# State scan of a four-layer network: one scan instruction over a whole image instead of two over its halves

## The chip, the cores and the metric

The kernel runs on one core of a Trainium2 chip. The metric is the device time of one execution in microseconds (us). Three runs of the kernel before gave 5059.32, 5066.79 and 5072.86 us; the median is 5066.79. A separate, profiled execution gave the page and the trace from which all durations below are read.

Engine names as in the profile: PE is the matrix engine (PEld its weight loads), DVE the vector engine, ACT the scalar engine with the activation functions, POOL the general engine, SP the engine that here does nothing but issue DMA transfers. "SPq" is SP's queue of issues; ACT and POOL issue some transfers too. L863 is line 863 of the kernel.

## What is computed

The reference is a network of four layers on an input of 8 images, 384 channels, 32 x 32 pixels. The change touches layer 0, a bidirectional selective state scan, and the place where layer 1 of an image begins. Cut to that:

```python
u = silu(causal_conv4(u) + conv1d_b)                 # (B, L, C), L = 1024 pixels
delta = softplus(dt @ dt_proj_w.T + dt_proj_b)       # (B, L, C)
A = -exp(A_log)                                      # (C, 16)
deltaA = exp(delta[..., None] * A)                   # (B, L, C, 16)
deltaBu = (delta * u)[..., None] * Bm[:, :, None, :]
def step(h, inp):
    dA, dBu, c = inp
    h = dA * h + dBu
    return (h, einsum('bdn,bn->bd', h, c))
y = scan(step, 0, ...) + u * D_param
y = y * silu(z)
out = einsum('bld,od->blo', y, out_proj_w)
```

It is run once forward (`fwd`) and once on the flipped sequence (`bwd`); their sum, scaled, is added to x together with a gated 3 x 3 convolution. Layer 1 (a convolution block, linear attention and an MLP), layer 2 (seven depthwise convolutions) and layer 3 (a 13 x 13 depthwise convolution with a pointwise one) follow.

For each image and each direction there are 384 channels x 16 states x 1024 pixels of recurrence, `h = dA * h + dBu`.

## The kernel before

**Three stages.** The front of image 0 runs alone. Then comes the long stage, 4 ms of the 5: the scan of image b runs as a chain of rounds, and between the rounds the kernel puts pieces of other jobs, the front of image b+1 (`front`: norm, input projection, convolutions, delta) and layer 1 of image b-1 (`layer1`). Last come layer 1 of image 7 and the layers 2 and 3 for all images.

**The scan, `scan(b)`.** A tile has 128 partitions: 32 channels x 4 states. The unit of work is (d, h, c): direction d, half h of the pixels (512 of 1024), chunk c of 128 channels. There are 2 x 2 x 3 = 12 units an image, for d = 1 with the halves in the order 1, 0. A unit has four rounds r, one for every four of the 16 states, so an image has 48 rounds, and a round has two tiles i. A tile is 128 x 1024 and holds two groups of 32 channels side by side, 512 pixels each. For a tile:

- ACT makes `da = exp(dlt * neg_a)` (L846), once for each group, since the factor per partition differs: two instructions on 512 columns. `da` has N_DA = 4 buffers.
- DVE makes `du = vr * bct` (L851), one instruction on 1024 columns into PSUM; `bct` holds the rows B and C of four states for one half.
- DVE runs the recurrence with `tensor_tensor_scan` (L863), once for each group, from `da` and `du` into `hs` (N_HS = 8 buffers). In the first half it starts from 0; in the second it starts from a state kept in `carry`.
- in the first half, DVE copies the last state of both groups into `carry` (L868).
- POOL multiplies `hs` by the row C in place (L872).

**The sums, `sums`.** PE sums the four states of a channel with the matrix `selt`: four 32-column products a round, one for each group, into the PSUM bank `acc` (L552 for the first, L557 for the others). There is one such bank; ACT fills it with `y0` at the start of a unit (L803). In the profile each fp32 product is two records. The sums of round n are put into the program in round n+2, so two rounds wait in the list `late`; at the end of an image the list is emptied (`for un in late`). After round 3 of a unit ACT copies `acc` and stores it as `yf` (d = 0, L816, L817), or DVE multiplies it by `zr` (L819) and POOL issues the store to `g_d` (d = 1, L820). For d = 1, `y0` is what d = 0 stored.

**Loads of the scan.** All go through SP: for a unit `dlt` and `vr` in two tiles each, each tile in two transfers of 256 KB, one for a group (L792), with N_REP = 6 buffers of one tag; `y0` (L832), `zr` (L835), and `bct` (L778) whenever the half or the direction changes. A load waits in SP's queue until its buffer is free.

**Jobs between the rounds.** `jobs` holds for each job a cost and the rounds from which and to which it runs. After each round the kernel takes pieces (up to the next `yield`) of the job that is furthest behind, until none is. Layer 1 of image b may run from round `(b + 1) * rounds` to round `(b + 2) * rounds`; its first piece, which loads weights and inputs, is taken 8 rounds before the scan of image b ends. `layer1` begins with the out projection: for h = 1 and then h = 0 it loads `xx` and `g`, and multiplies (`op<-g,wo`). Each engine works through its instructions in the order that the scheduler of the kernel's language gives them; the program order is their priority.

Of the kernel before, what the change touches and what calls it, by code (L numbers as in the profile page):

```python
# [10 lines left out]
FP = mybir.dt.float32  # L11
# [30 lines left out]
N_REP, N_DA, N_HS = 6, 4, 8  # L42
# [365 lines left out]
def _layers01(tc, nc, B, xv, x2_d, dram, ident, mean_w, eps5, eps6, one, half, minus1, vec, bns, bnt,  # L408
# [12 lines left out]
    with ExitStack() as ctx:  # L421
# [76 lines left out]
        carry = wp.tile([P, NC * NR, 4], FP, tag="carry", name="carry")  # L498

# [257 lines left out]
        newest = []  # L757

        def scan(b):

            units = [
                (d, h, c)
                for d in range(2) for h in ((0, 1) if d == 0 else (1, 0)) for c in range(NC)
            ]
            late = []

            def pairs(t):
                return t.rearrange("p (j n) -> p j n", n=HALF)

            def load_bc(k, r):  # L770
                d, h, _ = units[k]
                t = scanp.tile([P, 2, HALF], FP, tag="bct", name=f"bct_{b}_{d}_{h}_{r}", bufs=4)
                for o in range(2):
                    src = bass.AP(
                        bc_d.tensor, bc_d[b, d, o * NST + 4 * r, h * HALF].offset,
                        [[0, 32], [L, 4], [1, HALF]],
                    )
                    nc.sync.dma_start(t[:, o, :], src)  # L778
                return t

            def load(k, i):

                d, h, c = units[k]
                ts = []
                for src_d, n in ((dl_d, "dlt"), (v_d, "vr")):
                    t = scanp.tile([P, 2 * HALF], FP, tag="rep", name=f"{n}_{b}_{d}_{h}_{c}_{i}", bufs=N_REP)
                    for j in range(2):
                        src = bass.AP(
                            src_d.tensor, src_d[b, d, P * c + 32 * (2 * i + j), h * HALF].offset,
                            [[L, 32], [0, 4], [1, HALF]],  # L790
                        )
                        nc.sync.dma_start(t[:, bass.ts(j, HALF)], src)  # L792
                    ts.append(t)
                return ts

            def sums(k, r, hs, made, acc, y0, zt):
                d, h, c = units[k]
                cols = bass.ts(h, HALF)
# [3 lines left out]
                elif r == 0:  # L802
# [4 lines left out]
                        hs[j // 2][:, bass.ts(j % 2, HALF)],  # L807
# [6 lines left out]
                if d == 0:  # L814
                    yt = s2(f"yt_{b}_{h}_{c}")
                    nc.scalar.copy(yt, acc)  # L816
                    nc.scalar.dma_start(yfv[b][:, c, cols], yt)  # L817
                else:
                    nc.vector.tensor_mul(zt, acc, zt)  # L819
                    nc.gpsimd.dma_start(gv[b][:, c, cols], zt)  # L820

            bct = [load_bc(0, r) for r in range(NR)]
            now = [load(0, i) for i in range(2)]
            acc = y0 = zt = nxt = None
            for k, (d, h, c) in enumerate(units):
                cols = bass.ts(h, HALF)
                second = k % (2 * NC) >= NC
                for r in range(NR):
                    if r == 0:
                        acc = accp.tile([P, HALF], FP, tag="acc", name=f"acc_{b}_{d}_{h}_{c}")  # L830
                        y0 = s2(f"y0_{b}_{d}_{h}_{c}")
                        nc.sync.dma_start(y0, (udv if d == 0 else yfv)[b][:, c, cols])  # L832
                    if r == 1 and d == 1:
                        zt = s2(f"zr_{b}_{h}_{c}")
                        nc.sync.dma_start(zt, zv[b][:, c, cols])  # L835
                    if r == 1 and k + 1 < len(units):
                        nxt = [load(k + 1, 0)]
                    hs, made = [], []
                    way = slice(None) if d == 0 else slice(None, None, -1)
                    end = HALF - 1 if d == 0 else 0  # L840
                    for i in range(2):
                        dlt, vt = now[i]
# [476 lines left out]
```

## Time and profile before

The profiled execution has a span of 5036.6 us between its first and its last instruction, 30.2 us less than the median of the runs.

| Stage (us from the span's start) | length | PE busy | DVE busy | ACT busy | POOL busy | granted PE clock |
|---|---|---|---|---|---|---|
| scan of image 1 (667 to 1154) | 487 | 428.8 | 425.1 | 315.7 | 333.1 | 0.92 |
| scan of image 2 (1154 to 1655) | 501 | 444.1 | 424.5 | 322.6 | 332.3 | 0.94 |
| scan of image 4 (2158 to 2660) | 502 | 442.9 | 423.2 | 323.1 | 332.4 | 0.94 |
| scan of image 5 (2660 to 3159) | 499 | 442.8 | 422.9 | 323.1 | 332.5 | 0.94 |
| scan of image 6 (3159 to 3644) | 485 | 435.5 | 419.1 | 311.9 | 332.0 | 0.94 |
| after the scans (4080 to 5037) | 957 | 803.0 | 378.5 | 165.2 | 329.9 | 0.93 |

The windows go from the first `du` multiply of an image to that of the next; images 0, 3 and 7 stand with the prediction. Busy time is the union of an engine's instructions. Matmuls overlap and their ends are modelled, so PE's busy time is somewhat more than what it needs. A group line of the page gives line, engine, operation, out<-in with shapes, count, then busy us and mean ns of one instruction, then the idle time of the engine just before such instructions and what ended most of it. A wait line gives who waited for whom: us in total, how many times, longest.

Of the transfers, by issue: `dlt<-dl_d` and `vr<-v_d` x384 each, 256 KB, landing 4.6 and 5.0 us (median) after issue; `bct<-bc_d` x256, 256 KB, 3.9 us; `g_d<-zr` on POOL's queue x48, 256 KB, 5.3 us; `g<-g_d` x16, 768 KB, 7.8 us. The 16 DMA engines are busy 68% of the time in the middle of the run.

### The profile page before, as it was taken

Reading aid. Unit: us, or ns where it says so; the run is one execution under the profiler, and the core shown is the slowest. Engines: PE = TensorE matmul, PEld = TensorE weight load, DVE = VectorE, ACT = ScalarE, POOL = GpSimd, SP = SyncE. Lnnn points to the kernel's source line nnn. Section 1 sums busy time; section 2 is a strip of 40 time slices with the busy share of each in tenths; the row PEclk is TensorE's granted clock in tenths of the full one; section 3 lists DMA queues with packets and bytes.
Section 4 is the critical chain, followed back from the end, with each engine's and each line's share of the span. In section 5 each row is a group of like instructions: output and inputs, shape, how many; then the busy total and the mean of one; then the engine's idle time right before and its main releaser. Section 6 shows DMA issues by size and latency. Waiting matters only on the chain. (4 is left out here: it accounts for less than half of the span.)

```text
span 5036.6 us, 58480 instructions
## 1 busy us (share of the span) xinstructions
PE 4203.6 (83%) x20128; PEld 1781.9 (35%) x20128; DVE 3791.7 (75%) x3861; ACT 2637.3 (52%) x3738; POOL 2997.3 (60%) x1546
## 2 busy tenths in 40 slices
PE   6466588888888888889888989889888879978988
PEld 2121223333333233323332333333333324457457
DVE  1599999878987898789978997889898830157256
ACT  2456555774577457745774577567645622200212
POOL 1477577666766676667666666766776760033058
PEclk9676799899989998999899989998988989999999
DMA  7976557577657765776577657765763672389798
GB/s 205 278 226 221 182 190 214 179 216 195 214 175 214 196 213 174 213 195 214 177 214 191 216 179 212 210 214 180 176 192 127 160 156 78 68 162 251 210 207 172
DMA packets 543120, 965.28 MB, mean 192 GB/s; under 512 B 56568, under 2 KB 220904, under 8 KB 542824
## 3 DMA queue, kind: packets, MB, share of 16 engines
q1 hardware_dynamic: 401648, 663.89, 45.1%
q0 software_dynamic: 58048, 205.76, 15.8%
q10 hardware_dynamic: 83128, 91.90, 6.7%
q8 instruction: 159, 2.61, 0.2%
q14 instruction: 137, 1.12, 0.1%
HBM read 726.36 MB, written 234.98 MB: 191 GB/s over the span
## 5 line engine op out<-in xcount | busy, mean ns | idle before, releaser
L872 POOL TENSOR_TENSOR hs<-hs,bct 128x1024 f32<-128x1024 f32 x768 | 2414.6, 3145 | 945.5 <-DVE carry L868 438.6
L846 ACT ACTIVATE da<-dlt,neg_a 128x512 f32<-128x512 f32 x1536 | 1035.8, 715 | 1041.4 <-DVE hs L863 970.7
L863 DVE TENSOR_TENSOR_SCAN hs<-da,carry,du 128x512 f32<-128x512 f32 x768 | 942.4, 1266 | 191.8 <-PE acc L557 139.1
L851 DVE TENSOR_TENSOR du<-vr,bct 128x1024 f32<-128x1024 f32 x768 | 1033.0, 1345 | 31.4 <-DMA vr<-v_d 19.6
L863 DVE TENSOR_TENSOR_SCAN hs<-da,du 128x512 f32<-128x512 f32 x768 | 900.9, 1208 | 129.3 <-PE acc L557 54.4
L557 PE MATMUL acc<-hs,selt 128*32 128x512 f32 x2304 | 541.5, 660 | 134.8 <-POOL hs L872 134.7
L539 PE MATMUL mf<-ln,w 128*128 128x512 f32 x1152 | 549.2, 623 | 27.6 <-DMA w<-w_d 17.0
L1172 PE MATMUL mo<-hm,w 128*128 128x512 f32 x1152 | 532.7, 600 | 15.0 <-DVE xx L1139 15.0
L552 PE MATMUL acc<-hs,selt 128*32 128x512 f32 x768 | 420.9, 643 | 58.6 <-POOL hs L872 50.3
L539 PE MATMUL in<-xn,win 128*128 128x512 f32 x576 | 292.4, 646 | 64.6 <-DMA win<-in_inproj_t 29.0
L539 PEld LDWEIGHTS mf<-ln,w 128*128 128x128 f32 x1152 | 222.8, 200 | 339.4 <-issue 271.9
L1172 PEld LDWEIGHTS mo<-hm,w 128*128 128x128 f32 x1152 | 214.5, 190 | 309.1 <-issue 281.3
L846 ACT ACT_TABLE_LOAD x235 | 301.5, 1283 | 7.1 <-DMA dw_i<-h_d 2.4
L330 PE MATMUL cv_a<-xt_a,tp_a 128*32 128x256 f32 x3072 | 183.8, 387 | 55.1 <-issue 26.6
L1142 POOL DMA_DIRECT2D x_d<-xx x48 | 56.5, 1179 | 282.1 <-DVE xx L1139 274.9
L539 PE MATMUL op<-g,wo 128*128 128x512 f32 x288 | 158.3, 701 | 73.8 <-DMA g<-g_d 73.8
L557 PE MATMUL dw<-dw_i,t3b 96*32 96x512 f32 x1056 | 203.9, 637 | 16.5 <-DMA dw_i<-h_d 16.1
L330 PE MATMUL cv_b<-xt_b,tp_b 128*32 128x256 f32 x3072 | 184.5, 393 | 38.3 <-DVE xt_b L306 25.7
L306 DVE COPY xt_b<-xt_b 32x2496 f32<-32x2496 f32 x96 | 149.2, 1554 | 68.0 <-DMA xt_b<-xp_d 63.4
L539 PEld LDWEIGHTS in<-xn,win 128*128 128x128 f32 x576 | 111.6, 204 | 237.1 <-issue 165.0
L330 PEld LDWEIGHTS cv_a<-xt_a,tp_a 128*32 128x32 f32 x3072 | 159.6, 138 | 79.6 <-issue 34.7
L330 PEld LDWEIGHTS cv_b<-xt_b,tp_b 128*32 128x32 f32 x3072 | 155.7, 139 | 67.4 <-issue 41.1
(196 smaller groups left out, 5758.8 us busy)
## 6 DMA issues: line engine op xcount, KB each, us to landing
dlt<-dl_d SPq DMA_DIRECT2D x384, 256.0 KB, 4.6
vr<-v_d SPq DMA_DIRECT2D x384, 256.0 KB, 5.0
bct<-bc_d SPq DMA_DIRECT2D x256, 256.0 KB, 3.9
ut<-u_d SPq DMA_DIRECT2D x192, 257.5 KB, 5.7
lc_i<-xn_d SPq DMA_DIRECT2D x192, 228.8 KB, 5.4
dw_i<-h_d SPq DMA_DIRECT2D x192, 228.8 KB, 5.4
w<-w_d SPq DMA_DIRECT2D x64, 576.0 KB, 6.1
w<-in_w SPq DMA_DIRECT2D x64, 576.0 KB, 5.7
```

The costliest lines, as they stand in the source:

```text
L306: nc.vector.tensor_copy(xt[at[e] : at[e] + e * H, :, 0 : RL - e - (e - 1)], xt[at[0] : at[0] + e * H, :, e : RL - (e - 1)],)
L330: nc.tensor.matmul(ps[H * e : H * (e + 1), 0:BW], tp[:, c, :].rearrange("p (j t) -> p j t", t=KT)[:, :, t], rhs, start=(t == 0), stop=(t = ...
L539: product = nc.tensor.matmul(ps, w[:, k, m * P : (m + 1) * P], rhs[k] if isinstance(rhs, list) else rhs[:, k, :], start=(k == 0), stop=(k ...
L552: first = product()
L557: tc.keep_in_program_order(product())
L846: nc.scalar.activation(da[:, bass.ts(j, HALF)], dlt[:, bass.ts(j, HALF)], AF.Exp, scale=neg_a[:, g, r : r + 1],)
L851: nc.vector.tensor_mul(pairs(du), pairs(vt), bct[r][:, 0:1, :].to_broadcast([P, 2, HALF]),)
L863: nc.vector.tensor_tensor_scan(t[:, s][:, way], da[:, s][:, way], du[:, s][:, way], k_c if second else 0.0, ALU.mult, ALU.add,)
L872: made.append(nc.gpsimd.tensor_mul(pairs(t), pairs(t), bct[r][:, 1:2, :].to_broadcast([P, 2, HALF])))
L1142: nc.gpsimd.dma_start(x2v[m, :, h * (H // 2) : (h + 1) * (H // 2), PADW + b * (W + PADW) : PADW + b * (W + PADW) + W,], rows(o),)
L1172: nc.tensor.matmul(acc[m], wb[:, f, m * P : (m + 1) * P], hm, start=(i == 0 and f == 0), stop=(i == FF // C - 1 and f == NC - 1),)
```

## The change

- A unit is now (d, c, q): direction, chunk c of 128 channels, and q, which half of that chunk's channels (64). It covers all 1024 pixels. There are again 12 units of four rounds with two tiles.
- A tile holds one group of 32 channels x 4 states over the whole image. One exp of 1024 columns and one scan of 1024 columns, always started from 0, replace two of 512; `carry` and its copies go.
- The exp writes into the `hs` tile, and the scan and POOL's multiply work on it in place; `da` goes. N_HS is 9 instead of 8, N_REP 5 instead of 6. `bct` tiles are twice as long.
- Loads: `dlt` and `vr` come as one transfer of 512 KB a tile. The four of the next unit are requested one in round 1 and the others in round 3, between the instructions that free their buffers. `bct` is loaded once a direction.
- The bank `acc` has the 64 channels' first half of the pixels in partitions 0 to 63 and their second half in 64 to 127, so `y0`, `zr`, `yf` and `g` move in two transfers of 64 partitions each (`fetch`, `keep`).
- The list of sums that wait, now `late_sums`, lives on from image to image and is emptied after the last image only.
- Layer 1 of an image may start 3 rounds later. It loads both halves of `xx` in its first piece, then `g` of the first two chunks, then `g` of the last chunk, and then multiplies for h = 1 and h = 0. In the last image the second piece is taken 3 rounds before the end.

```diff
-N_REP, N_DA, N_HS = 6, 4, 8
+N_REP, N_HS = 5, 9
...
-        newest = []
+        newest, late_sums = [], []
...
+            units = [(d, c, q) for d in range(2) for c in range(NC) for q in range(2)]
+            def halves(t_d, k):
+                _, c, q = units[k]
+                lo = P * c + 64 * q
+                return [t_d[b][lo : lo + 64, bass.ts(h, HALF)] for h in range(2)]
+            def fetch(t, t_d, k):
+                for h, src in enumerate(halves(t_d, k)):
+                    nc.sync.dma_start(t[64 * h : 64 * h + 64, :], src)
+            def keep(t_d, k, t, queue):
+                for h, dst in enumerate(halves(t_d, k)):
+                    queue.dma_start(dst, t[64 * h : 64 * h + 64, :])
...
+            def load(k, n):
+                d, c, q = units[k]
+                i, o = divmod(n, 2)
+                t = scanp.tile([P, L], FP, tag="rep", name=f"{('dlt', 'vr')[o]}_{b}_{d}_{c}_{q}_{i}", bufs=N_REP)
+                src_d = (dl_d, v_d)[o]
+                src = bass.AP(
+                    src_d.tensor, src_d[b, d, P * c + 64 * q + 32 * i, 0].offset, [[L, 32], [0, 4], [1, L]],
+                )
+                nc.sync.dma_start(t, src)
+                return t
...
-                        hs[j // 2][:, bass.ts(j % 2, HALF)],
+                        hs[j % 2][:, bass.ts(j // 2, HALF)],
...
                     for i in range(2):
+                        dlt, vt = now[2 * i : 2 * i + 2]
+                        t = scanp.tile([P, L], FP, tag="hs", name=f"hs_{b}_{k}_{r}_{i}", bufs=N_HS)
+                        nc.scalar.activation(t, dlt, AF.Exp, scale=neg_a[:, 4 * c + 2 * q + i, r : r + 1])
+                        if r == NR - 1 and more:
+                            nxt.append(load(k + 1, 2 * i + 1))
+                        du = accp.tile([P, L], FP, tag="du", name=f"du_{b}_{k}_{r}_{i}")
+                        nc.vector.tensor_mul(du, vt, bct[r][:, 0, :])
+                        if i == 0 and r == NR - 1 and more:
+                            nxt.append(load(k + 1, 2))
+                        if i == 0 and len(late_sums) > 1:
+                            late_sums.pop(0)()
+                        if i == 0 and k == per and r == 0:
+                            bct[NR - 1] = load_bc(1, NR - 1)
+                        nc.vector.tensor_tensor_scan(
+                            t[:, way], t[:, way], du[:, way], 0.0, ALU.mult, ALU.add,
                         )
+                        made.append(nc.gpsimd.tensor_mul(t, t, bct[r][:, 1, :]))
...
+                    late_sums.append(partial(sums, k, r, hs, made, acc, y0, zt))
...
-            for un in late:
-                sums(*un)
+            if b == B - 1:
+                while late_sums:
+                    late_sums.pop(0)()
...
             for h in (1, 0):
-                xh, gh = a6(f"xx_{b}_{h}"), a6(f"g_{b}_{h}")
-                nc.sync.dma_start(xh, x1v[b][:, :, bass.ts(h, HALF)])
-                nc.sync.dma_start(gh, gv[b][:, :, bass.ts(h, HALF)])
-                xx[h] = xh
-                yield 0
+                xx[h] = a6(f"xx_{b}_{h}")
+                nc.sync.dma_start(xx[h], x1v[b][:, :, bass.ts(h, HALF)])
+            yield 0
+            gh = {}
+            for h in (1, 0):
+                gh[h] = a6(f"g_{b}_{h}")
+                nc.sync.dma_start(gh[h][:, 0 : NC - 1, :], gv[b][:, 0 : NC - 1, bass.ts(h, HALF)])
+            yield 0
+            for h in (1, 0):
+                nc.sync.dma_start(gh[h][:, NC - 1, :], gv[b][:, NC - 1, bass.ts(h, HALF)])
+            yield 0
+            for h in (1, 0):
                 for m in range(NC):
...
-            jobs.append([seconds[b], 310, (b + 1) * rounds + 0, (b + 2) * rounds + 0, 0])
+            jobs.append([seconds[b], 310, (b + 1) * rounds + 3, min((b + 2) * rounds + 3, B * rounds), 0])
...
-                if i == rounds - 8:
+                if i == rounds - 8 or (b == B - 1 and i == rounds - 3):
                     next(seconds[b])
```

## The prediction

> **What bounds the kernel now.** I read the page's totals first, then a table of windows cut at the images (from the first du multiply of an image to that of the next), then the groups, then who waited for whom, and last the timelines at one change of image.
>
> ```profile
> span 5036.6 us, 58480 instructions
> ...
> PE 4203.6 (83%) x20128; PEld 1781.9 (35%) x20128; DVE 3791.7 (75%) x3861; ACT 2637.3 (52%) x3738; POOL 2997.3 (60%) x1546
> ```
>
> ```profile
> 146.00:667.00 521.00, 300.44 (x1079) 96.29 (x1078) 470.30 (x491) 275.06 (x381) 330.80 (x171) 0.72 0.69 216
> 1655.00:2158.00 503.00, 444.10 (x1696) 168.33 (x1696) 425.22 (x423) 323.04 (x447) 333.49 (x149) 0.94 0.68 199
> 3644.00:4080.00 436.00, 365.24 (x1263) 145.56 (x1260) 379.46 (x384) 233.10 (x341) 313.87 (x112) 0.90 0.53 150
> ```
>
> The columns are the window, its length, then busy time of PE, PEld, DVE, ACT and POOL, the granted clock, the DMA share and GB/s. The three rows are images 0, 3 and 7. Image 0 is DVE's (470 of 521 us, PE 300). In image 3, as in 1 to 6, PE (444) and DVE (425) are nearly level and both stand idle some 60 to 80 us. So the middle of the run is bound by two engines that take turns, and I ask at each saving who holds the path.
>
> ```profile
> L872 POOL TENSOR_TENSOR hs<-hs,bct 128x1024 f32<-128x1024 f32 x768 | 2414.6, 3145 | 945.5 <-DVE carry L868 438.6
> L846 ACT ACTIVATE da<-dlt,neg_a 128x512 f32<-128x512 f32 x1536 | 1035.8, 715 | 1041.4 <-DVE hs L863 970.7
> L863 DVE TENSOR_TENSOR_SCAN hs<-da,carry,du 128x512 f32<-128x512 f32 x768 | 942.4, 1266 | 191.8 <-PE acc L557 139.1
> L851 DVE TENSOR_TENSOR du<-vr,bct 128x1024 f32<-128x1024 f32 x768 | 1033.0, 1345 | 31.4 <-DMA vr<-v_d 19.6
> L863 DVE TENSOR_TENSOR_SCAN hs<-da,du 128x512 f32<-128x512 f32 x768 | 900.9, 1208 | 129.3 <-PE acc L557 54.4
> ```
>
> Of the waits in images 1 to 6 (667 to 3644 us), three decide:
>
> ```profile
> DVE hs L863 <- PE acc L557: 169.5, 54, 12.2
> ```
>
> ```profile
> PE op L539 <- DMA g<-g_d: 43.0, 5, 10.9
> PE acc L557 <- POOL hs L872: 40.7, 18, 2.8
> ```
>
> The scans wait 28 us an image for an hs buffer that PE's sums have not released. PE waits for the states only 7 us an image (the row above), but at each change of image it waits for g. The timeline of PE there:
>
> ```profile
> 1658.97 1.92 PE L557 MATMUL acc<-hs,selt 128*32 128x512 f32 x4 [2.79 <-POOL hs L872]
> ...
> 1667.84 5.31 PE L539 MATMUL op<-g,wo 128*128 128x512 f32 x12
> 1680.77 7.43 PE L539 MATMUL op<-g,wo 128*128 128x512 f32 x12 [7.62 <-DMA g<-g_d]
> ```
>
> The last sums of image 2 are emptied at its end, their g is written out (the issue on POOL is at 1662.01, SP's g load goes out at 1674.5), and PE stands behind that load.
>
> **Scans and carries (DVE).** Removed: 1536 scans of 512 and 384 carry copies (184 ns each); added: 768 scans of 1024. No row shows a scan of 1024. It can't cost more than two of 512 without carry, 2416 ns, and not less than that minus one whole smallest instruction, 2416 - 184 = 2232. DVE's instructions on 128x1 take 143 to 153 ns, which is nearly all fixed cost, so I take 2416 - 150 = 2266. Now a tile's two scans occupy
>
> ```profile
> 1653.01 2.45 DVE L863 TENSOR_TENSOR_SCAN hs<-da,carry,du 128x512 f32<-128x512 f32 x2
> 1655.50 1.23 DVE L851 TENSOR_TENSOR du<-vr,bct 128x1024 f32<-128x1024 f32 x1
> 1656.86 2.33 DVE L863 TENSOR_TENSOR_SCAN hs<-da,du 128x512 f32<-128x512 f32 x2
> ```
>
> 2.45 or 2.33 us, mean 2.39; less 2.27 is 0.12 us. A copy moves the next start by 0.08 us on half of the tiles, 0.04 more: 0.16 us a tile, 123 us over 768 tiles, 15.4 an image. What of it is on the path? I followed the chain of waits back from the last scan of each image, by the rule of the page's part 4: scans hold 150 us of the chain in image 0, 59 to 86 (mean 74) in images 1 to 6, 115 in image 7, of 237 us of scans each: 63%, 31% and 49%. So 15.4 x 0.63 + 6 x 15.4 x 0.31 + 15.4 x 0.49 = 9.7 + 28.6 + 7.5 = **46 us**. Bounds: 17 (images 0 and 7 alone) and 123 (all of it). The du multiply and POOL's multiply keep size and count.
>
> What speaks against it: POOL's multiply was released by the carry copy on half of the tiles (438.6 us of its waits) and is now released by the scan, just as the next du starts. Second-half tiles have no copy today, and there du takes 1.23 us (the fence above) while POOL's multiply stretches from 2.36 to 3.2 or 3.3: du goes first. I take nothing, and no loss as the bound.
> The Trainium skill ("SBUF — State Buffer", section "SBUF: two separate sides") says that a DVE instruction with two SBUF inputs and a GpSimd instruction exclude each other for their whole length, whoever starts first. By that rule alone a du that now came second would lose up to a whole POOL multiply, 384 x 2.36 = 906 us; the rows of the second halves show the other order, and the sum goes by them.
>
> **Exps (ACT).** 1536 of 512 become 768 of 1024. The Gelu rows, 475 ns at 256 and 687 at 512, give 0.83 ns a column, so 715 + 512 x 0.83 = 1139 instead of 1430: 0.29 us a tile, 223 us of ACT. On the same chains exps hold 22, 84 (six images together) and 25 us; 131 x 0.2 = 27 us. But they now write into hs, not into da, so exp n waits until PE's sums have freed tile n-9. In the trace a scan starts 13.3 us (median) after those sums, 4.7 at the tenth percentile, 3.2 at least, and the exp needs 1.2 of it. The 13.8 us by which exps lead today shrink. I take half, **13 us**; bounds 0 and 27.
>
> **Late sums and the shifted start.** The sums of an image's last two rounds no longer drain at its end, and the out projection starts 3 rounds later (some 31 us at 502/48 us a round), with g loaded in two parts ahead. PE's waits for g are 73.8 us in 8 places; the tail's one is 15.5, which leaves 58.3 for seven changes of image, 8.3 each. The chain runs on into DVE, whose L958 waits there 38.5 us in six images. I take all **58 us**. Bounds: 0 (another wait takes its place) and 58 plus the 3.6 us that PE waits for POOL's last tiles at this change (0.79 + 2.79), times 7: 83.
>
> **Tail.** In the last image the out projection of half 1 (18 records, 0.43 us apart in the timeline, 7.7 us) ran between the last sums, while half 0 waited for g. Now both wait for the last channel group: +7.7, less about 2 for a smaller last load (g 768 KB lands in 7.8 us, y 256 KB in 3.3 to 6.0): **+6 us**, bounds 0 and 8. Squeezing image 6's second layer into 45 rounds instead of 48 costs nothing while PE idles 70 of 436 us in image 7; 3/48 of its load (310 units, 3 for six records of 0.43 us: 17 us) would show if that idle time went.
>
> **Moves of data.** Per image SP issues 146 loads now and 100 then, the same bytes: dlt and vr in one piece of 512 KB, y and z in two pieces. Stores of yf and g are two pieces each: 48 more issues on POOL at 583 ns, 28 us, hidden in POOL's 170 idle us per image, and 48 on ACT's queue. With five rep buffers, dlt of a unit's second tile waits for the du of the last round's first tile, as vr of the second tile does today; that one landed a median of 10.7 us before its use and 3.6 at the tenth percentile, and dlt is wanted some 2.5 us sooner. So next to nothing, and behind it on SP stand the next vr and g. Buffers of N_HS and N_DA cost no time by themselves.
>
> **The sum.** -46 - 13 - 58 + 6 = -111 us, on a span of 5036.6: 4926. The median of the runs, 5066.8, lies 30.2 above that span, and that stays: **4956 us**. By the bounds: -123 - 27 - 83 + 0 = -233 and -17 + 8 = -9.
>
> **Rivals.** *All of it lands* (13%): PE's lag in images 1 to 6 comes from late DVE and ACT steps, so a lighter DVE frees PE too: 5066.8 - 233 = 4834. For it: DVE is 85% busy. Against: scans wait for PE, not PE for scans. *PE keeps the pace* (15%): images 1 to 6 stay as they are, the g wait is followed by a wait for an a6 buffer that the layer before still holds: 5066.8 - 17 - 4 + 6 = 5052. For it: POOL waits there 7.94 us for such a buffer. *Exps tied to the sums* (12%), the slower side: an exp that queues behind ACT's table load, Gelu and load back (1.28 + 0.69 + 1.28, some 3.3 us, and 1.2 of its own) comes too late where its slack is under 4.7 us, a tenth of the tiles. If a fifth of the tiles come 1.5 us late, 154 x 1.5 = 230, less 111: 5186. It decides from 74 tiles on, where 74 x 1.5 = 111. Against: the slack after n-9 today. That the long scan saves nothing is the lower bound of the first term.
>
> **How the numbers follow.** My forecast has 60%, with a range of its own of 4900 to 5010. About 0.3% (15 us, 5052 to 5082) is what a measurement can tell from no change. Faster: 60 + 13 and a third of PE's case, 78%; within 0.3%: 8%, most of PE's case; slower: 14%. The range leaves out half of the fastest case and most of the slow one: 4870 to 5080.
>
> **What would show it.** A scan row of 128x1024 near 2.27 us x768 and an exp row near 1.14; no carry row; DVE near 3600 us busy and ACT near 2410; the g wait of PE gone but for the tail, about 20 us there; image 0 near 511 and images 1 to 6 near 485 us. Wrong would be: long waits "DVE hs <- ACT" or "ACT <- PE acc", du far above 1.35 us, or g waits that reappear under another name.

## The result and the profile after

The changed kernel takes 5292.8 us (median of 4 runs, 5287.9 to 5294.0), the kernel before on the same chip 5069.8 (4 runs, 5059.3 to 5076.3). The ratio is 1.0439, 95% interval 1.0424 to 1.0454: **slower by 223 us**, where 111 us less were forecast.

The totals of the changed kernel's page:

```profile
span 5292.1 us, 55997 instructions
...
PE 4259.5 (80%) x20128; PEld 1782.4 (34%) x20128; DVE 3804.7 (72%) x2709; ACT 2439.9 (46%) x2936; POOL 3003.9 (57%) x1594
```

DVE runs 1152 instructions fewer and is busy for 3805 us, 13 more than before. ACT lost 197 us of work, of the 223 forecast. The groups say why DVE lost nothing (busy time and mean ns of one, then the idle time before them by cause):

```profile
L856 POOL TENSOR_TENSOR hs<-hs,bct 128x1024 f32<-128x1024 f32 x768 | 2400.5, 3126 | 1166.2 <-DVE hs L853 1048.3 <-issue 47.0 <-PE pj L537 10.6
L853 DVE TENSOR_TENSOR_SCAN hs<-hs,du 128x1024 f32<-128x1024 f32 x768 | 1754.6, 2285 | 392.4 <-ACT hs L842 334.8 <-PE dw L555 2.7 <-DVE du L846 1.4
L846 DVE TENSOR_TENSOR du<-vr,bct 128x1024 f32<-128x1024 f32 x768 | 1186.9, 1545 | 142.1 <-DMA vr<-v_d 122.2
L842 ACT ACTIVATE hs<-dlt,neg_a 128x1024 f32<-128x1024 f32 x768 | 851.8, 1142 | 421.1 <-DMA dlt<-dl_d 208.0 <-PE acc L555 194.3 <-issue 10.6
...
L537 PE MATMUL op<-g,wo 128*128 128x512 f32 x288 | 147.3, 653 | 124.7 <-DMA g<-g_d 124.7
```

The scan takes 2285 ns and the exp 1142 ns, close to the 2266 and 1139 that were worked out. But the du multiply, whose size did not change, went from 1345 to 1545 ns: 768 x 0.2 = 154 us. The scans and carries fell from 942.4 + 900.9 + 70.7 = 1914 us to 1754.6, which is 159 us. The one ate the other. And PE's wait for g rose from 73.8 to 124.7 us, where 58 of the 73.8 were to go.

The windows of images 0, 3 and 7 (length; busy time of PE, PEld, DVE, ACT, POOL; granted clock; DMA share; GB/s), cut at the first du multiply of each image as in the prediction:

```profile
173.00:668.00 495.00, 283.69 (x1005) 91.27 (x1006) 429.86 (x333) 220.37 (x249) 331.38 (x163) 0.68 0.68 214
1728.00:2271.00 543.00, 453.57 (x1698) 169.79 (x1697) 429.96 (x279) 303.22 (x351) 334.07 (x154) 0.90 0.63 184
3876.00:4323.00 447.00, 378.68 (x1300) 150.39 (x1299) 383.71 (x242) 212.86 (x249) 317.50 (x118) 0.91 0.52 147
```

Cut in this way, the whole difference of the two spans, 255.5 us, can be placed: the first du multiply starts 28 us later (173.7 against 145.8), image 0 is 27 us shorter, images 1 to 6 are 231 us longer together, image 7 is 11 and the rest 13 us longer. (The profiled execution of before was some 30 us under its median; hence 255 and not 223.) The shorter image 0 is no gain of the shorter scans: a unit now covers the whole image, so the first one needs both halves of the first front, and work of that front which ran between the rounds before now runs ahead of them. Image 1 begins at 668.0 us, before at 667.2. What the change cost, it cost where the layers run beside the scan: in image 3, 40 us, with PE busy 9 and DVE 5 us more. So most of it is waiting. The waits of images 1 to 6 (us in total, times, longest):

```profile
DVE hs L853 <- ACT hs L842: 295.8, 79, 21.7
ACT L842 <- PE acc L555: 167.1, 69, 7.2
...
ACT sq L641 <- DMA xi<-in_x: 123.5, 5, 26.8
...
PE ms_s L611 <- ACT sq L641: 107.7, 5, 22.3
DVE du L846 <- DMA vr<-v_d: 103.5, 15, 15.1
...
PE op L537 <- DMA g<-g_d: 96.3, 5, 21.4
```

Three things stand there that were not there before. Scans wait 296 us for their exps; exps wait for PE's sums; and five times, once an image, PE and ACT stand some 20 us behind `xi`, the input of the next front. In images 1 to 6 of the kernel before, these waits were:

```profile
DVE hs L863 <- ACT da L846: 12.6, 12, 1.5
...
PE ms_s L613 <- ACT sq L643: 10.6, 5, 3.2
...
ACT sq L643 <- DMA xi<-in_x: 9.4, 3, 4.0
```

The timeline of image 3 shows what a wait for `xi` drags along (start, length, and in brackets the idle time before it):

```profile
2191.39 2.37 POOL L1130 DMA_DIRECT2D x_d<-xx  x2
...
2194.55 1.16 POOL L1130 DMA_DIRECT2D x_d<-xx  x1 [0.80 <-issue]
...
2214.04 0.37 SPq L637 DMA_DIRECT2D xi<-in_x  x1
...
2219.45 1.67 ACT L641 ACTIVATE sq<-xi 128x512 f32<-128x512 f32 x3 [23.90 <-DMA xi<-in_x]
...
2220.13 1.17 PE L611 MATMUL ms_s<-sq,mean_w 128*32 128x128 f32 x16 [21.30 <-ACT sq L641]
...
2223.61 2.29 DVE L853 TENSOR_TENSOR_SCAN hs<-hs,du 128x1024 f32<-128x1024 f32 x1 [20.71 <-ACT hs L842]
```

The second layer (`layer1`), three rounds later now, stores its last result (`x_d<-xx`, three transfers) from an a6 buffer that the next front's `xi` is to take; a6 is the tag of the seven large tiles that the fronts and the layer share. The last of the three stores lands at 2213.89, 19 us after its issue. SP stands at the load of `xi` until then, 119.6 us in five times (20.1 in the kernel before), and vr and dlt of the next unit go out behind it (2214.5 to 2215.8). ACT stands at the squares of `xi`, with the exps of the scan queued behind them; PE stands at the mean, with the sums behind it; and so DVE and POOL stop too. One buffer that comes free too late stops all engines for 20 us.

### The profile page after: what moved, and what is told of

Its sections match the earlier page's. It is cut to its first block, busy times and chain, and to the rows that moved or that the text cites. A ratio compares the mean times of both kernels' runs of the same rounds, so it can differ in the third digit from the quotient of the medians.

```text
span 5292.1 us, 55997 instructions
## 1 busy us (share of the span) xinstructions
PE 4259.5 (80%) x20128; PEld 1782.4 (34%) x20128; DVE 3804.7 (72%) x2709; ACT 2439.9 (46%) x2936; POOL 3003.9 (57%) x1594
## 5 line engine op out<-in xcount | busy, mean ns | idle before, releaser
L853 DVE TENSOR_TENSOR_SCAN hs<-hs,du 128x1024 f32<-128x1024 f32 x768 | 1754.6, 2285 | 392.4 <-ACT hs L842 334.8
L846 DVE TENSOR_TENSOR du<-vr,bct 128x1024 f32<-128x1024 f32 x768 | 1186.9, 1545 | 142.1 <-DMA vr<-v_d 122.2
L842 ACT ACTIVATE hs<-dlt,neg_a 128x1024 f32<-128x1024 f32 x768 | 851.8, 1142 | 421.1 <-DMA dlt<-dl_d 208.0
L555 PE MATMUL acc<-hs,selt 128*32 128x512 f32 x2304 | 468.5, 679 | 118.9 <-POOL hs L856 118.9
L550 PE MATMUL acc<-hs,selt 128*32 128x512 f32 x768 | 435.0, 658 | 109.1 <-POOL hs L856 74.2
L537 PE MATMUL op<-g,wo 128*128 128x512 f32 x288 | 147.3, 653 | 124.7 <-DMA g<-g_d 124.7
L550 PEld LDWEIGHTS acc<-hs,selt 128*32 128x32 f32 x768 | 61.6, 114 | 371.2 <-issue 235.7
```

The costliest lines, as they stand in the source:

```text
L537: product = nc.tensor.matmul(ps, w[:, k, m * P : (m + 1) * P], rhs[k] if isinstance(rhs, list) else rhs[:, k, :], start=(k == 0), stop=(k ...
L550: first = product()
L555: tc.keep_in_program_order(product())
L842: nc.scalar.activation(t, dlt, AF.Exp, scale=neg_a[:, 4 * c + 2 * q + i, r : r + 1])
L846: nc.vector.tensor_mul(du, vt, bct[r][:, 0, :])
L853: nc.vector.tensor_tensor_scan(t[:, way], t[:, way], du[:, way], 0.0, ALU.mult, ALU.add,)
```

## The experiments

Each kernel starts from before or from after with the edit shown. "Before" ran on the same chip in each set; its median lay between 5066.7 and 5076.4.

### The shifted start

First the shift alone, in the kernel before:

```diff
-jobs.append([seconds[b], 310, (b + 1) * rounds + 0, (b + 2) * rounds + 0, 0])
+jobs.append([seconds[b], 310, (b + 1) * rounds + 3, min((b + 2) * rounds + 3, B * rounds), 0])
```

> The kernel before with one part of the change alone: layer 1 of an image may start, and must end, 3 rounds later. Theory S (the shift: the next front still begins 8 rounds before the scan's end and now finds its a6 buffers held by layer 1 of the image before, some 20 us an image in the trace of after): 5150 to 5220 us against 5070, with a wait of ACT sq for xi near 20 us an image. Theory E (exps tied to the hs buffers) or theory R (five rep buffers) as the main cause: within 0.5% of before, 5045 to 5095.

5290.6 us, ratio 1.0433 (1.0408 to 1.0459): by itself the shift costs as much as the whole change, 224 us, and more than was expected. In images 1 to 6 the wait for `xi` has come up:

```profile
PE ms_s L613 <- ACT sq L643: 108.7, 6, 21.9
```

Then the same with an eighth a6 buffer, for which room was made with fewer t2 and im buffers (smaller tiles of the fronts and layers):

```diff
-N_A6, N_T2, N_S2, N_W, N_IM = 7, 9, 3, 4, 8
+N_A6, N_T2, N_S2, N_W, N_IM = 8, 7, 3, 4, 7
```

> The kernel before with the second layer three rounds later (5290.6 us by itself) and eight a6 buffers instead of seven; to make room, seven t2 and seven im buffers instead of nine and eight. If the shift costs because the next front's image waits for an a6 buffer that the second layer holds, 60 to 200 us come back: 5090 to 5230 us, and the wait of xi for the xx stores goes. If it costs because loads and stores collide at the change of image (theory C), the eighth buffer gives nothing: 5260 to 5340 us, the fewer t2 and im buffers costing up to 40.

```profile
PE ms_s L613 <- ACT sq L643: 3.5, 3, 2.2
```

5240.0 us (ratio 1.0336). The wait for `xi` goes, from 108.7 to 3.5 us, so it is the a6 buffer that made it. Only 51 us come back, short of the 60 to 200 expected. The fewer t2 and im buffers may take some of it; seven t2 and six im cost 64 us in the changed kernel (below), but seven and seven were not tried alone here. So 171 of the shift's 224 us stand without the wait for `xi`. The trace shows part of them: scans wait 73 us for their exps, which was 13 us before. What the rest is stays open.

In the changed kernel, two of the three rounds undone:

```diff
-(b + 1) * rounds + 3, min((b + 2) * rounds + 3, B * rounds)
+(b + 1) * rounds + 1, min((b + 2) * rounds + 1, B * rounds)
```

> The changed kernel with the second layer one round later than an image instead of three; the late sums and all else stay. In the kernel before, three rounds more alone cost 224 us. Theory S (the start of the second layer three rounds later makes its loads, stores and buffers collide with the next front and the next unit's loads): two of the three rounds are undone, so 80 to 200 us come back, 5093 to 5213 us; the out projection now waits for g at the change of image, some 10 us each, which is inside that range. Theory E (what costs is that exps write into hs and have lost their lead): the shift is no cause of its own here, within 40 us of the changed kernel, 5253 to 5333 us.

5210.0 us (ratio 1.0272): 83 us come back, and PE's wait for the squares falls from 107.7 to 12.8 us. The wait for g does not go; it is 114.6 us in images 1 to 6, where it was 96.3.

Instead of the layer, the fronts were moved:

```diff
-jobs.append([front(b), 100, max(0, (b - 1) * rounds - 8), b * rounds - 8 - 1, 0])
+jobs.append([front(b), 100, max(0, (b - 1) * rounds - 5), b * rounds - 6, 0])
```

> The changed kernel with the fronts moved too: each starts and ends 3 rounds later, so that front and layer 1 stand to each other as they did before. Theory S: the wait of ACT sq for xi goes (107 us of PE's waits in images 1 to 6) and the time falls by 80 to 150 us from 5293, to 5140 to 5210. Theories E and R: 5270 to 5310.

5241.4 us (ratio 1.0332): 51 us come back, short of the 80 to 150 expected; PE's wait for the squares is 46.4 us.

And the changed kernel with its sums emptied at each image's end and the layer where it was:

```diff
-if b == B - 1:
-    while late_sums:
-        late_sums.pop(0)()
+while late_sums:
+    late_sums.pop(0)()
...
-(b + 1) * rounds + 3, min((b + 2) * rounds + 3, B * rounds)
+(b + 1) * rounds + 0, min((b + 2) * rounds + 0, B * rounds)
```

> The changed kernel with the sums emptied at each image's end and the second layer started where it was before: only the long scan, the exps into hs, the split by channel group halves and five rep buffers are left of the change. Theory S: all of the shift's loss comes back, 5050 to 5130 us. Theory E: exps into hs cost 173 us in the kernel before and nothing is left here to pay for them but the shorter scans (at most 123 us), so 5120 to 5290 us. Where it lies under 5052 us the scan part of the change is a gain by itself; above 5082 us it is a loss by itself.

5232.8 us (ratio 1.0319): 60 us come back, and what is left of the change, the long scan with exps into hs, the new units and five rep buffers, costs 164 us against before. So the shift is one cause among several, and their costs do not add: 224 alone in before, 51 to 83 in the changed kernel.

### The scan and the du multiply

To see the long scan by itself, before got one scan of 1024 a tile, without the carry, and nothing else:

```diff
-for j in range(2):
-    s = bass.ts(j, HALF)
...
-    nc.vector.tensor_tensor_scan(
-        t[:, s][:, way], da[:, s][:, way], du[:, s][:, way],
-        k_c if second else 0.0, ALU.mult, ALU.add,
-    )
-if not second:
-    nc.vector.tensor_copy(
...
+nc.vector.tensor_tensor_scan(
+    t[:, way], da[:, way], du[:, way], 0.0, ALU.mult, ALU.add,
+)
```

> The kernel before with one scan of 1024 in place of a tile's two of 512, and no carry: the second group of a tile runs on from the first and the second half of an image starts from zero, so that part of the recurrence is not the reference's; sizes, buffers, exps into da, order and the second layer's start stay. The prediction's step alone: scan row near 2285 ns, no carry row, 46 us less (17 to 123), 4944 to 5050 us, if the du multiply stays at 1345 ns. Theory L (with no carry the multiply on POOL starts at the scan's end, and where another DVE instruction stands between the scan and the next du, du comes second and takes 3 us): du 1500 to 1560 ns, DVE busy unchanged near 3790 us, time within 40 us of before or above, 5040 to 5110.

```profile
L860 DVE TENSOR_TENSOR_SCAN hs<-da,du 128x1024 f32<-128x1024 f32 x768 | 1754.0, 2284 | 426.9 <-PE acc L557 303.0 <-ACT da L846 40.7 <-PE c L552 15.9
L851 DVE TENSOR_TENSOR du<-vr,bct 128x1024 f32<-128x1024 f32 x768 | 1142.3, 1487 | 49.8 <-DMA vr<-v_d 28.4
```

5116.4 us, ratio 1.0079 (1.0053 to 1.0105): 40 us slower. The du multiply takes 1487 ns. Why, the timelines show. In the kernel before, on a tile of a first half (the lines of DVE and POOL):

```profile
1687.75 1.22 DVE L863 TENSOR_TENSOR_SCAN hs<-da,du 128x512 f32<-128x512 f32 x1
1688.89 0.73 DVE L958 SCALAR_TENSOR_TENSOR xx<-op,rsm,xx 128x512 f32<-128x512 f32 x1
1689.53 1.21 DVE L863 TENSOR_TENSOR_SCAN hs<-da,du 128x512 f32<-128x512 f32 x1
1690.78 0.17 DVE L868 COPY carry<-hs 128x2 f32<-128x2 f32 x1
...
1690.85 1.23 DVE L851 TENSOR_TENSOR du<-vr,bct 128x1024 f32<-128x1024 f32 x1
1691.09 3.19 POOL L872 TENSOR_TENSOR hs<-hs,bct 128x1024 f32<-128x1024 f32 x1 [1.27 <-DVE carry L868]
```

and in the changed kernel:

```profile
1785.82 2.29 DVE L853 TENSOR_TENSOR_SCAN hs<-hs,du 128x1024 f32<-128x1024 f32 x1
1788.02 0.73 DVE L946 SCALAR_TENSOR_TENSOR xx<-op,rsm,xx 128x512 f32<-128x512 f32 x1
1788.18 2.35 POOL L856 TENSOR_TENSOR hs<-hs,bct 128x1024 f32<-128x1024 f32 x1 [0.27 <-DVE hs L853]
1788.66 2.96 DVE L846 TENSOR_TENSOR du<-vr,bct 128x1024 f32<-128x1024 f32 x1
```

A layer's step on DVE (here L958, L946) stands between two instructions of the scan. Before, it stood between the scans or ahead of the copy; POOL was released by the copy, 0.24 us after du had begun, and it was POOL that was stretched (3.19 us). Now POOL is released by the scan, while DVE is still at the layer's step. POOL comes first and takes 2.35 us, and du is the one that waits (2.96). Counted over the trace of before: where a layer's step stands between the last scan of a tile and the next du, 1 of 77 du multiplies starts while POOL's runs on first halves, and on second halves, which have no copy, 45 of 51, these 1.3 us longer in the mean. On first halves the step came behind the copy 8 times; six of these du multiplies took 3.5 us. In the changed kernel 152 of all 768 du multiplies start while POOL's runs, in the one before 59.

So a copy of one column was put behind the long scan, for POOL to wait for:

```diff
+nc.vector.tensor_copy(
+    carry[:, c * NR + r, 2 * i : 2 * i + 1], t[:, 2 * end + 1 : 2 * end + 2] if d == 0 else t[:, 0:1],
+)
```

> As the kernel with one scan of 1024 a tile (5116.4 us; du 1487 ns; the second group runs on from the first and the second half starts from zero, so that part of the recurrence is not the reference's), and after each scan a copy of one column, which the multiply on POOL has to wait for, as the carry copy made it on half of the tiles. Theory L (the copy lets DVE's next instruction start before POOL): du falls to 1230 to 1300 ns, some 150 us of DVE, at the price of 768 copies near 150 to 190 ns, and the time falls by 20 to 90 us, to 5026 to 5096. If du stays near 1490 ns, the copy is not what protected it, and the time rises by up to 60 us.

```profile
L851 DVE TENSOR_TENSOR du<-vr,bct 128x1024 f32<-128x1024 f32 x768 | 994.0, 1294 | 22.5 <-DMA vr<-v_d 21.4 <-issue 0.6 <-DMA bct<-bc_d 0.5
...
L863 DVE COPY carry<-hs 128x1 f32<-128x1 f32 x768 | 116.5, 152 | 21.0
```

5078.4 us, 38 less; du falls to 1294 ns. More instructions, less time. The ratio to before is 1.0004 (0.9991 to 1.0018): with du shielded, DVE is 51 us less busy than before (3740.6), and the time is the same. Image 0, where DVE is the bound, did not get shorter either (524 us; 521 before, 520 without the copy). Scans wait longer in images 1 to 6 for sums to release an hs buffer, 272 us where it was 169.5:

```profile
DVE hs L860 <- PE acc L557: 272.4, 65, 12.2
```

The same copy in the changed kernel with the start one round later:

```diff
+held = wp.tile([P, 8], FP, tag="held", name="held")
...
+o = 2 * r + i
+e = L - 1 if d == 0 else 0
+nc.vector.tensor_copy(held[:, o : o + 1], t[:, e : e + 1])
 made.append(nc.gpsimd.tensor_mul(t, t, bct[r][:, 1, :]))
```

> The changed kernel with the second layer one round later than an image instead of three (5210.0 us, du 1513 ns), and after each scan a copy of one column, for which POOL's multiply has to wait. Theory L: du falls to 1230 to 1320 ns, DVE some 60 us less busy. In the kernel before the same copy gave 38 us; 20 to 60 us are expected here, 5150 to 5190. Theory O (the order of the steps among each other decides, not DVE's busy time): du falls all the same, and the time lies anywhere within 70 us of 5210, up or down. Under 5060 it would beat the kernel before.

```profile
L848 DVE TENSOR_TENSOR du<-vr,bct 128x1024 f32<-128x1024 f32 x768 | 1001.7, 1304 | 24.1 <-DMA bct<-bc_d 13.4 <-DMA vr<-v_d 10.7
```

5110.7 us, ratio 1.0077 (1.0054 to 1.0101): 99 us less than without the copy, more than the 20 to 60 expected and more than DVE's busy time fell (3817 to 3766). How much of the 99 is du, and how much the new order that comes with any edit (below), is not split. With the shift cut to one round and the copy back, 182 of the 223 us are gone.

### The exps and their buffers

Before with exps written into hs and scanned in place, with nine and with twelve buffers (da and hs had four and eight):

```diff
-da = scanp.tile([P, 2 * HALF], FP, tag="da", name=f"da_{b}_{k}_{r}_{i}", bufs=N_DA)
+t = scanp.tile([P, 2 * HALF], FP, tag="hs", name=f"hs_{b}_{k}_{r}_{i}", bufs=N_HS)
...
-t[:, s][:, way], da[:, s][:, way], du[:, s][:, way],
+t[:, s][:, way], t[:, s][:, way], du[:, s][:, way],
```

> The kernel before with the exps written into the hs tile and the scan in place, no da tiles, nine hs buffers; halves, carries and all else as before. Theory E (exps wait for PE's sums and lose their lead over the scans): 5110 to 5200 us, with waits of ACT for PE acc of 30 us an image or more and of DVE for ACT of 20 or more. Theories S and R: 5045 to 5095.

> The kernel before with exps written into hs and scanned in place, and twelve hs buffers, which take the room of the four da and eight hs buffers. With nine it took 5239 us, 173 more than before. If what cost there is that an exp must wait for the sums nine tiles back (theory E), twelve give most of the lead back: 5060 to 5130 us. If it is the scan reading and writing the same tile, or the fixed order on the engines, more buffers do not help: 5200 to 5260 us.

5239.3 us with nine (ratio 1.0336), 5103.2 with twelve (1.0067): three buffers give back 136 us. With twelve, 34 are left. That the number of hs buffers counts is shown; the expected way, by exps that wait for sums, is not what the traces show. In images 1 to 6 the exps, with the table loads ahead of them, wait 142 us for sums with nine and 119 with twelve, but the scans wait 160 us for their exps in both, and over the whole run the median time from the end of an exp to the start of its scan is 10 us in both. What went is du's wait for vr; with nine and with twelve buffers (668 to 3700 us):

```profile
DVE du L851 <- DMA vr<-v_d: 115.4, 14, 12.7
...
DVE du L851 <- DMA vr<-v_d: 7.1, 7, 1.8
```

Over images 1 to 6 it is 129.5 and 7.1 us, and these images are 135 us longer with nine. Why vr comes late with nine was not tried.

The changed kernel with one hs buffer fewer:

```diff
-N_REP, N_HS = 5, 9
+N_REP, N_HS = 5, 8
```

> The changed kernel with eight hs buffers instead of nine, all else the same. Theory E: each buffer fewer takes some 45 us (136 us between nine and twelve in the kernel before), 30 to 130 us more than the changed kernel, 5320 to 5420. If the lead is no cause in the changed kernel, 5270 to 5310.

5354.5 us (ratio 1.0552), 62 more, as expected if the lead of the exps (the time by which they end ahead of their scans) were the cause. The trace does not show it so: in images 1 to 6 the scans wait 306 us for their exps, where it was 296, and the exps, with the table loads ahead of them, 290 us for sums, where it was 284. And a new order of the same work alone moved the kernel before by as much (below). With more buffers it could not be shown either. Eleven need room, which was taken from t2 and im; the control has the smaller t2 and im alone:

```diff
-N_A6, N_T2, N_S2, N_W, N_IM = 7, 9, 3, 4, 8
+N_A6, N_T2, N_S2, N_W, N_IM = 7, 7, 3, 4, 6
...
-N_REP, N_HS = 5, 9
+N_REP, N_HS = 5, 11
```

> The changed kernel with eleven hs buffers instead of nine; to make room, seven t2 and six im buffers instead of nine and eight; the start of the second layer stays three rounds later. Theory E (exps wait for the sums nine tiles back): in the kernel before, nine to twelve gave back 136 us, so two of three such steps give 60 to 120 us here: 5170 to 5230 us, and DVE's wait for the exp falls well under 300 us. Theory S alone (the shift): within 30 us of the changed kernel, 5260 to 5320 us.

> The changed kernel with seven t2 and six im buffers instead of nine and eight, and nine hs buffers: the control for the one with eleven, which took 5444.5 us. If the fewer t2 and im buffers are what cost there, 5440 to 5560 us, and the difference to 5444.5 is what two more hs buffers give (60 to 120 by theory E). If they cost nothing, 5270 to 5320 us, and more hs buffers would be harmful by themselves.

> As the one before (eleven hs buffers), with the second layer one round later than an image instead of three, which alone gave 83 us. If both causes stand beside each other their gains add: 5293 - 83 - 60 to 120, so 5090 to 5150 us. If they are one and the same stall seen from two sides, 5180 to 5215 us. Under 5052 us it would beat the kernel before.

5444.5 us with eleven, 5356.9 for the control with nine, and 5320.8 with eleven and the start one round later. No expectation held: two more buffers cost 88 us where 60 to 120 were to be gained, the control fell between its two cases, and the last lies far over its 5090 to 5215. Exps do wait less for sums (182 us in the control, 120 with eleven, over the whole run). ACT then waits longer at steps of the front and the layer for PE, and in images 1 to 6 the scans wait longer for ACT (328 us in the control, 431 with eleven). Why PE is late there was not tried further.

Five rep buffers instead of six, in before:

```diff
-N_REP, N_DA, N_HS = 6, 4, 8
+N_REP, N_DA, N_HS = 5, 4, 8
```

> The kernel before with five rep buffers instead of six, nothing else. Theory R (loads of the next unit come too late with five): 5100 to 5200 us, with new waits of DVE du for vr and of ACT for dlt of 10 us an image or more. Theories S and E: 5045 to 5095.

5098.7 us, ratio 1.0066 (1.0041 to 1.009): 32 us, put down as "next to nothing". In its trace du waits 101 us for vr in images 1 to 6, where it was 1.3. Five buffers alone do not decide that wait: in the changed kernel it is 103.5 us, and with the layer one round later, still with five buffers, 0.6.

### The order of the same work

The kernel with one scan a tile also got one exp of 1024 a tile, still into da:

```diff
-for j in range(2):
-    g = 4 * c + 2 * i + j
-    nc.scalar.activation(
-        da[:, bass.ts(j, HALF)], dlt[:, bass.ts(j, HALF)], AF.Exp,
-        scale=neg_a[:, g, r : r + 1],
-    )
+nc.scalar.activation(da, dlt, AF.Exp, scale=neg_a[:, 4 * c + 2 * i, r : r + 1])
```

> As the kernel with one scan a tile, and also one exp of 1024 a tile in place of two of 512 (the second group takes the first one's decay). Exps still write into da and keep their lead. The prediction's step: ACT about 220 us less busy, 13 us less on the path (0 to 27), so 0 to 27 us under the kernel with one scan alone. If ACT's order among the layer's steps matters more than its length, within 10 us of it.

5217.8 us (ratio 1.0285): 101 us *more* than with the two exps, with ACT 158 us less busy. Neither case of the expectation had that. The round that lost most is the 38th of images 2 to 5, 32.5 us in place of 15.3. In image 3 the timeline has there:

```profile
2099.17 2.74 PE L1158 MATMUL mo<-hm,w 128*128 128x512 f32 x6
2101.74 5.31 PE L539 MATMUL mf<-ln,w 128*128 128x512 f32 x12
2106.89 2.74 PE L1158 MATMUL mo<-hm,w 128*128 128x512 f32 x6
2109.56 1.13 PE L736 MATMUL dt<-xd,wdt 24*128 24x512 f32 x4
...
2119.60 0.62 PE L552 MATMUL acc<-hs,selt 128*32 128x512 f32 x1
...
2120.77 2.29 DVE L855 TENSOR_TENSOR_SCAN hs<-da,du 128x1024 f32<-128x1024 f32 x1 [16.78 <-PE acc L557]
```

PE is busy all the time (49.00 of the 49 us from 2071 to 2120), but with the front and the layer: from 2071.2 to 2119.6 no sums stand in its order, and DVE waits 16.78 us for an hs buffer. In the kernel with two exps the sums around the same rounds of image 3 lie 10 to 12 us apart (2050.3, 2061.9, 2073.0 and 2083.0). The scheduler writes the order of each engine anew for each kernel, and with other exps it wrote another one.

What another order costs when the work stays the same was asked with a single number, the cost that `jobs` holds for the layer (310), in the kernel before, once down and once up (305 and 315):

```diff
-jobs.append([seconds[b], 310, (b + 1) * rounds + 0, (b + 2) * rounds + 0, 0])
+jobs.append([seconds[b], 305, (b + 1) * rounds + 0, (b + 2) * rounds + 0, 0])
```

> The kernel before with one number of the planner changed: the second layer's cost is given as 305 instead of 310, so that its pieces are taken a little later among the rounds; instructions, sizes and buffers are the same. Theory O (this order is a fitted one, and any other order of the same work costs): 30 to 150 us more, 5100 to 5220. If the order hardly matters, 5050 to 5090 us, and the loss by the longer exps needs another cause.

> The kernel before with the second layer's cost given to the planner as 315 instead of 310, so that its pieces are taken a little earlier; the work is the same. With 305 it took 63 us more. If the order of before is a fitted one, this side loses too: 20 to 120 us, 5090 to 5190. If only lateness of the layer costs, as in the kernel with three rounds more, this side is not slower: 5030 to 5080.

With 305 it takes 5137.6 us, ratio 1.0133 (1.0114 to 1.0153); with 315, 5083.5, ratio 1.0035 (1.0024 to 1.0046). Both sides lose, 63 us where the layer's pieces come later and 15 where they come earlier, which is just under the 20 to 120 expected. With 305 the wait for `xi` is back in images 1 to 6:

```profile
PE ms_s L613 <- ACT sq L643: 79.5, 5, 16.9
```

No version beat the kernel before.

## Why the prediction was wrong

Of the three gains in the sum none reached the time, and two of the steps that were to bring them, the start three rounds later and the exps into hs, cost time instead.

**"Scans and carries", -46: wrong on du, and on the path share.** The scan (2285 ns) and the work saved on scans and carries (159 us) were near what was put down. "I take nothing" for du was the step that failed. Its evidence, "there du takes 1.23 us ...: du goes first", was read from a place where du follows the scan at once. Where a layer's step lies between, POOL goes first on 45 of 51 such tiles without a copy. Measured: +154 us of du. And the share on the path was too high as well: with du shielded, DVE was 51 us less busy, which by the prediction's share (46 of 123) is worth 19 us, and the time did not change (ratio 1.0004). Image 0, to which 63% were given, did not get shorter with the long scan alone.

The rule that I weighed there, from the Trainium skill, "SBUF — State Buffer", section "SBUF: two separate sides" (two such instructions exclude each other, and whichever starts first holds the other up), describes what the two timelines show: 2.96 us of du beside 2.35 of POOL, or 1.23 beside 3.19. What the rule leaves open, and what decided, is which of the two starts first.

**"Exps", -13: a risk was named, the term had the wrong sign.** That an exp now waits for the sums nine tiles back, and that the lead shrinks, was there. Half the gain was kept all the same. In place of a gain, nine buffers in place cost the kernel before 173 us and twelve 34. In the changed kernel the median lead of the exps over their scans fell from 13.8 to 7.8 us in images 1 to 6, and a tenth of them have none. But what three more buffers took away in the kernel before was du's wait for vr, which this step did not name; that the lost lead is what costs is argued, not shown.

**"Late sums and the shifted start", -58: wrong in sign.** PE's wait for g did not go but grew by 51 us, and the shift made a new wait, of 108 us, behind `xi`; alone in the kernel before it cost 224 us. A wait for an a6 buffer was named in the rival "PE keeps the pace", but at the out projection and as something that only takes a gain away. It came at the other end of the layer, at the next front, and cost more than was there to win. The step did not follow a late layer to its end: it asked what the shift removes at the layer's first load and not who takes the layer's last buffer. That wait is not the whole cost of the shift: with an eighth a6 buffer it was gone, and 171 us stayed. Why g is later than before was not tried by itself. (The load of g after which PE stands goes out at 1674.78, not at 1674.5; nothing hangs on it.)

**"Moves of data", about 0: one term missed.** Five rep buffers cost 32 us in before. That the scan starts 28 us later, after both halves of the first front, was not foreseen either; it happens in every kernel with the new units (the first du at 173 to 196 us) and in none of the others (146 to 152). In the changed kernel it cost nothing by the start of image 1, since image 0 is shorter by as much.

**"Tail", +6: not shown.** What comes after the scans is 13 us longer, but in the other kernels made from before, whose tail was not touched, it is 6 to 31 us longer too. So the 13 us can't be put down to the new loads.

**The rivals.** "Exps tied to the sums" (5186, to decide from 74 tiles on) came nearest: 79 scans wait for their exps, 3.7 us each and not 1.5. By its own sum with these numbers, 5066.8 - 111 + 79 x 3.7 = 5248, it is 45 us short, and it is no exact account: the 111 us did not come, and a part of these waits is the stall behind `xi` seen from DVE (20.71 us in the timeline), not the lost lead. "All of it lands" fell where the scans were shortened and the time did not follow.

**What is left open.** Of the 223 us, 83 went with two rounds of the shift and 99 more with the copy. The last 42 stand beside the waits of scans for exps (269 us in images 1 to 6 of that kernel) and of PE for g (122 us); no run splits them. The parts are not independent: 224 (shift), 173 (exps in place, nine buffers) and 32 (rep), each alone in before, are 429. Every edit also changes the order of the instructions, and that alone was worth 15 and 63 us; so a difference of such a size between two kernels (38 for the copy in before, 51 for the eighth buffer, 62 for one hs buffer) does not by itself show its cause. That the order of the sums cost the merged exps 101 us is shown at one place in the rounds, and for the rest argued from the two kernels with another cost number. The lower granted clock (0.90 in image 3, before 0.94) goes with the longer waits; whether it cost anything by itself was not tried.

## What to carry to other kernels

Where several engines work through fixed orders with few buffers to spare, a saving on one of them is worth what its waits leave of it: ask for each moved step which buffer it frees, who takes that buffer next, and what stands behind the taker in its queue. A small instruction can be worth its time by whom it releases and when; before taking one away, look at what waited for it, and at all neighbours that can stand there, not one. Measure also what a new order of the same work costs (here 15 and 63 us for one number of the planner) before a difference of that size is put down to an instruction.

## What was not expected of the hardware

Two multiplies of 128x1024 that both read SBUF, du on DVE and hs on POOL, take 1.23 and 3.2 us when DVE is first, and 2.96 and 2.35 us when POOL is: the later one waits about as long as the first still runs (1.73 us for POOL's 1.87, 0.83 for du's 0.99). A copy of 128x1 takes 152 ns, but the next instruction on DVE starts 0.07 to 0.08 us after its start (the copy at 1701.03, du at 1701.10 in the kernel with the long scan and the copy), so 768 of them cost less than their busy time of 117 us says. One scan of 1024 saves 2 x 1208 - 2285 = 131 ns against two of 512. And the store `x_d<-xx`, 256 KB, lands a median of 15.8 us (before) and 17.3 us (after) after its issue, where the other stores of 256 KB take 2.7 to 6.2 us. It is this store that `xi` waited for. It writes pieces of 32 numbers where `x_d<-xr` of the same size (4.7 and 4.1 us) writes pieces of 512; whether that is the reason was not tried.
